# Two layers of graph attention: how the attention denominators are inverted, which buffers setup and FF1 use, and when the rows are loaded

## The chip, the cores and the metric

The kernel runs on one core of one Trainium2 chip. Its engines each run their own queue of instructions: TensorE (PE; its weight loads are listed apart as PEld), VectorE (DVE), ScalarE (ACT), GpSimd (POOL) and SyncE (SP), which here only issues DMA transfers. The time is the device time of one execution in microseconds; the number compared is the median of several runs. Besides, one execution is recorded by the hardware profiler: all durations of single instructions below come from that one.

## The reference

Two layers are applied in turn to `x`, 64 sequences of 256 rows with 256 features, with a 256 x 256 adjacency of zeros and ones for each. Cut to what matters:

```python
# layer 0: two graph attentions, then norm, FF with relu, norm
def _gat(h, adj, W, a):
    Wh = h @ W
    e  = leaky_relu(Wh @ a[:256] + swapaxes(Wh @ a[256:], 1, 2), 0.2)
    return softmax(where(adj > 0, e, NEG), axis=1) @ Wh
h = layernorm(x + _gat(_gat(x, adj, W1, a1), adj, W2, a2))
x = layernorm(h + relu(h @ w_ff1 + b_ff1) @ w_ff2 + b_ff2)

# layer 1: relational attention, 8 heads of 32, then norm, FF with gelu, norm
attn = softmax(q @ k.T / sqrt(32))                 # per head
out  = sum_r (attn * (adj == r)) @ (x @ Wv[r])     # r = 0, 1 occur
x = layernorm(x + out @ Wo + bo)
x = layernorm(x + gelu(x @ W1 + b1) @ W2 + b2)
```

The part that the change is mostly about is the softmax of layer 1. The kernel does not divide the weights by their sum; it multiplies the weighted values by the inverse of the sum at the end.

## The kernel before

**Tiling.** A pair of sequences (G = 2) is one unit of work: 512 rows, kept as four tiles of 128 rows, or with the features on the 128 partitions and the 512 rows along the columns. There are 32 pairs (NG). A general path stands behind a check at the end (`checks`, `good`, `bad`) and is not entered with these inputs; the sums kept in `low`, `lowg`, `high` and `other` feed that check.

**Turns.** The pairs are in a pipeline of three. In `turn(y, x, z)` (32 times, with y, y + 1, y + 2) pair y goes through layer 1, pair x = y + 1 through the feed-forward of layer 0, and pair z = y + 2 through the two graph attentions. In the second last turn there is no z, in the last neither x nor z; there the code goes another way (`to_features` on TensorE in place of `normed_features`; the last products of pair 30 are cut in pieces, called by `piece()` inside the last turn).

**Order.** TensorE and SP follow the order of the program text (`manual_schedule`); a planner orders VectorE, ACT and POOL by its own estimate of costs, each queue then running strictly in its order. `behind(...)` puts what it encloses after a marked instruction of the same engine.

**Attention of layer 1.** A pair has four quads of heads, (sequence b, group m), two for each sequence. `weighted` (L988 to L999) makes scores, exponentials `e`, masked exponentials `ea` and the row sums `es`. `applied` accumulates values in the PSUM tile `po` (L1009) and the sums in `zo` (L1012). The stationary operand of the latter is a matrix of ones with 32 columns, so the 32 partitions of one head in `zo` hold the same number: of each 32 rows of `zo` only one is distinct. `divided` (L1017, L1018), after the second quad of a sequence, takes the reciprocal of all 128 x 512 elements and multiplies `po` by it into `oT`, which the output product (L760) reads. `noted` (L1025) sums the reciprocals on ACT into a column of `low`. In a turn with a z, the projection of pair z (L707) stands on TensorE between the output products of the two sequences.

**FF1 of layer 1.** `hidden_seven` (L833 to L850) computes the product in seven quarter products, Strassen fashion. Partial results from one PSUM bank are copied by ACT (L839) into a tile `cp` (slots of tag `ea`), and VectorE adds the other bank to it into the quarter of `h1` where it belongs (L843); then gelu works on `h1` in place.

**Buffers.** A tile belongs to a tag with a number of slots (`bufs`); a new tile waits until the oldest in its tag has been read. `y`, the rows of a pair, has five slots and is loaded at the head of `load_x`, before the eight transfers of `xq`, in the turn before the pair becomes z. The scores `s` of the graph attentions have two slots. At setup `columns` (L491 to L496) loads short vectors as rows on ACT's queue, transposes them on TensorE and copies them out; it is called twice, for the attention vectors (`ga`) and for ten others (`cols`), with rows in the one slot of tag `rz`. Three bias rows (L503, L628) are loaded by SP into that same slot, one after the other, and added by POOL.

**Other lines that the prediction names.** L457, L459: rows and adjacency of the first two pairs. L577 to L580: POOL's sums of weights. L588: products that fold a shift into a bias. L595: scaling of weights on POOL. L646 and L647: transposes of `to_features` on TensorE and ACT's copies of them. L661, L680: the transposes of `normed_features` on VectorE and its transfers. L699: `checked`. L716: the score rows. L730 to L736: the masked softmax of the graph attention. L749: its first sums. L777: the power in the normalisation. L798, L892: the feed-forward of layer 0. L913, L918: the pieces of the last product and their additions. L1034: the transposition of `xq`. L1099: the store of the output.

## Time and profile before

| | us |
|---|---|
| median of 3 runs | 3161.23 |
| lowest, highest | 3158.11, 3163.35 |
| the profiled execution | 3159.55 |
| its span, first to last instruction | 3157.6 |
| mean granted TensorE clock in it | 0.991 |

From the page, the span in 40 equal slices of 79 us: each digit is the busy share of a slice in tenths, and PEclk the granted clock of TensorE in the same way.

```profile
PE   7999999999999999999999999999999999999997
...
DVE  3577777777777777777777777777777777777765
ACT  4355544545544545545545545545445555445442
POOL 2121111111111111111211111211111211111200
PEclk8999999999999999999999999999999999999998
DMA  5011111111111111111111111111111111111000
```

The middle of the kernel is even; the first slices and the last differ in every row. In the lists of groups, a row has the source line, the engine, the operation, the tiles written and read, their shapes and the count; then busy time and mean duration, then the idle time of the engine just before and what ended it. In a timeline a row begins with the start and the duration.

### The profile page before, as it was taken

To read this page: it belongs to the slowest core of one execution; us is meant where nothing else is said; L and a number is where in the kernel's file an instruction comes from. 1 tells how busy PE (TensorE), PEld (TensorE's weight loads), DVE (VectorE), ACT (ScalarE), POOL (GpSimd) and SP (SyncE) were. 2 spreads that over 40 slices of the span, in tenths; PEclk is the share of its full clock that TensorE was granted. 3 is DMA by queue.
4 is the path that set the end of the run, shared out by engine and by line. 5 is a ranking of instruction groups with operands and counts; after the bars stand their busy time and mean duration, and the time that the engine had idled before them with its cause. 6 is when DMAs were issued, how large, how long until landed. Compare 5 with 4: busy or idle time off the path is not lost. (4 is left out here: it accounts for less than half of the span.)

```text
span 3157.6 us, 50461 instructions
## 1 busy us (share of the span) xinstructions
PE 3097.2 (98%) x19120; PEld 2199.1 (70%) x19120; DVE 2329.8 (74%) x4146; ACT 1548.6 (49%) x3088; POOL 521.2 (17%) x757
## 2 busy tenths in 40 slices
PE   7999999999999999999999999999999999999997
PEld 5577766677766777666777666777666777666755
DVE  3577777777777777777777777777777777777765
ACT  4355544545544545545545545545445555445442
POOL 2121111111111111111211111211111211111200
PEclk8999999999999999999999999999999999999998
DMA  5011111111111111111111111111111111111000
GB/s 145 19 36 26 41 31 38 43 36 25 39 35 37 40 35 28 36 38 37 36 35 32 34 39 38 36 28 39 32 41 38 36 27 40 31 39 28 16 12 15
DMA packets 428536, 113.38 MB, mean 36 GB/s; under 512 B 364760, under 2 KB 427648, under 8 KB 428288
## 3 DMA queue, kind: packets, MB, share of 16 engines
q1 hardware_dynamic: 417952, 102.66, 14.7%
q10 hardware_dynamic: 9280, 6.39, 0.7%
q8 instruction: 153, 2.51, 0.3%
q0 software_dynamic: 1056, 1.05, 0.1%
q14 instruction: 95, 0.78, 0.1%
HBM read 57.04 MB, written 16.78 MB: 23 GB/s over the span
## 5 line engine op out<-in xcount | busy, mean ns | idle before, releaser
L798 PE MATMUL h1p<-hT,wf 128*128 128x512 f32 x992 | 450.6, 602 | 0.0
L892 PE MATMUL yfp<-wf,h 128*128 128x256 f32 x2048 | 447.3, 379 | 0.0
L892 PEld LDWEIGHTS yfp<-wf,h 128*128 128x128 f32 x2048 | 386.9, 190 | 51.9 <-issue 0.5
L781 ACT ACTIVATE y<-y,nm,rs 128x256 f32<-128x256 f32 x512 | 272.9, 597 | 237.9 <-DVE nm L778 237.9
L994 ACT ACTIVATE e<-sp 128x512 f32<-128x512 f32 x512 | 264.3, 602 | 250.4 <-PE sp L988 238.1
L996 DVE TENSOR_TENSOR ea<-e,aT 128x1024 f32<-128x1024 f32 x256 | 312.2, 1261 | 51.1 <-ACT e L994 47.0
L798 PEld LDWEIGHTS h1p<-hT,wf 128*128 128x128 f32 x992 | 180.8, 190 | 228.6 <-issue 183.3
L776 POOL TENSOR_SCALAR rs<-mv 128x4 f32<-128x4 f32 (+1 forms) x130 | 54.8, 421 | 1692.0 <-DVE mv L775 1686.4
L800 ACT ACTIVATE h<-h1p,cols 128x512 f32<-128x512 f32 x256 | 176.7, 690 | 222.3 <-PE h1p L798 222.3
L678 POOL COPY hT<-yt 32x256 f32<-32x256 f32 x248 | 241.2, 973 | 185.0 <-DVE yt L661 177.3
L1017 DVE RECIPROCAL rz<-zo 128x512 f32<-128x512 f32 x64 | 214.7, 3354 | 58.5 <-PE zo L1012 58.5
L661 DVE STREAM_TRANSPOSE yt<-y 128x256 f32<-128x256 f32 x368 | 162.6, 442 | 97.1 <-ACT y L781 88.6
L972 PE MATMUL vp<-wv,hT 128*128 128x512 f32 x480 | 214.0, 599 | 0.0
L774 DVE BATCH_NORM_STATS2 st<-y 128x6 f32<-128x256 f32 x512 | 195.8, 415 | 4.5
L843 DVE TENSOR_TENSOR h<-h1a,cp 128x512 f32<-128x512 f32 x192 | 130.9, 682 | 64.6 <-PE h1a L833 61.0
L988 PEld LDWEIGHTS sp<-q,k 32*128 32x128 f32 x2048 | 92.7, 184 | 109.6 <-issue 72.8
L961 ACT ACTIVATE q<-qp,cols 128x512 f32<-128x512 f32 x64 | 43.3, 677 | 255.1 <-PE qp L959 255.1
L709 ACT COPY xp<-xpp 128x260 f32<-128x260 f32 x128 | 47.9, 376 | 244.9 <-PE xpp L707 244.9
L972 PEld LDWEIGHTS vp<-wv,hT 128*128 128x128 f32 x480 | 88.7, 190 | 110.4 <-issue 103.2
L789 DVE TENSOR_TENSOR y<-y,rb 128x1024 f32<-128x1024 f32 (+1 forms) x130 | 162.1, 1248 | 3.3
L788 DVE TENSOR_TENSOR y<-y,rg 128x1024 f32<-128x1024 f32 (+1 forms) x130 | 157.3, 1211 | 9.2 <-PE h1T0p L646 3.6
L918 DVE TENSOR_TENSOR y<-yf,y 128x256 f32<-128x256 f32 x224 | 93.3, 417 | 84.8 <-PE yf L913 84.7
(209 smaller groups left out, 5762.3 us busy)
## 6 DMA issues: line engine op xcount, KB each, us to landing
hT<-yt SPq DMA_DIRECT2D x918, 32.0 KB, 1.9
y<-in_x_dram SPq DMA_DIRECT2D x32, 512.0 KB, 4.1
xq<-in_x_dram SPq DMA_DIRECT2D x240, 64.0 KB, 2.3
aq<-in_adj_dram SPq DMA_DIRECT2D x240, 64.0 KB, 2.4
out_dram<-y SPq DMA_DIRECT2D x30, 512.0 KB
hT<-yt ACTq DMA_DIRECT2D x186, 32.0 KB, 1.9
wf<-in_L_gnn_w_ff_dram SPq DMA_DIRECT2D x2, 1024.0 KB
w<-in_L_gnn_W_dram SPq DMA_DIRECT2D x2, 1024.0 KB
```

What stands on the lines that cost most here:

```text
L661: mark["transposed"] = nc.vector.transpose(yt[:, :, :, t].rearrange("p q k r -> p k q r"), xn[:, t].rearrange("p (k q c) -> p k q c", k=KB ...
L678: nc.gpsimd.tensor_copy(to, at)
L774: nc.vector.bn_stats(st[:, t, :], y[:, t, :])
L781: mark["normed"] = nc.scalar.activation(y[:, t, :], y[:, t, :], AF.Identity, bias=nm[:, t:t + 1], scale=rs[:, t:t + 1])
L789: nc.vector.tensor_add(y, y, b_[:, None, :].to_broadcast(list(y.shape)))
L798: nc.tensor.matmul(ps, wi[:, k, f * P:(f + 1) * P], hT[k], start=(k == 0), stop=(k == KB - 1))
L800: nc.scalar.activation(h1[:, f, :], ps, func, bias=bi[:, f:f + 1])
L892: nc.tensor.matmul(ps[:, i * F:(i + 1) * F], h1[:, k, t * P:(t + 1) * P], wo_[:, k, :], start=(k == 0), stop=(k == FB - 1))
L972: nc.tensor.matmul(ps, hT[k][:, t * P:(t + 1) * P], wvf[:, k, :], start=(k == 0), stop=(k == KB - 1))
L994: mark[f"exp{b * KB + m}"] = nc.scalar.activation(e[:, a, :], ps[a], AF.Exp, scale=isd)
L996: nc.vector.tensor_tensor(ea[:, a:a + 2, :], e[:, a:a + 2, :], ab[:, None, :].to_broadcast([P, 2, NB * N]), ALU.mult)
L1017: nc.vector.reciprocal(rz, zo)
```

## The change

`divided` no longer takes the reciprocal of all of `zo`. It transposes `zo` in blocks of 32 x 32, so that the equal rows of a head become equal columns; takes the reciprocal of the first column of each block, 16 in all, into a small tile `rq`; and transposes back, reading each of the 16 columns 32 times. The sum for the check is now an addition of `rq` to `low` (128 x 16) on POOL; `noted` is gone.

```diff
-    low = const.tile([P, NG * G], F32, name="low")
+    low = const.tile([P, KB * N // 32], F32, name="low")
+    nc.gpsimd.memset(low, 0.0)
...
     def divided(u, b, po, zo, oT):
         rz = work.tile([P, KB * N], F32, tag="rz", name=f"rz{u}_{b}", bufs=1)
-        nc.vector.reciprocal(rz, zo)
+        rq = work.tile([P, KB * N // 32], F32, tag="rq", name=f"rq{u}_{b}")
+        nc.vector.transpose(rz, zo)
+        nc.vector.reciprocal(rq, rz.rearrange("p (n r) -> p n r", r=32)[:, :, 0])
+        nc.gpsimd.tensor_add(low, low, rq)
+        nc.vector.transpose(rz.rearrange("p (n r) -> p n r", r=32),
+                            rq[:, :, None].to_broadcast([P, KB * N // 32, 32]))
         mark[f"divided{b}"] = nc.vector.tensor_tensor(
             oT[:, :, b * N:(b + 1) * N], po.rearrange("p (m n) -> p m n", m=KB),
             rz.rearrange("p (m n) -> p m n", m=KB), ALU.mult)
-        return rz
-
-    def noted(u, b, rz):
-        nc.scalar.activation(rz, rz, AF.Identity, accum_out=low[:, u * G + b:u * G + b + 1])
```

Setup tiles get buffers of their own: the rows of `ga` lie in tag `k`, those of `cols` in tag `q`, and the three bias rows side by side in `v`. Of the pair of copies in `to_features`, the second goes to VectorE. The scores `s` of the first two pairs lie in tag `e`, and `s` itself has one slot; in the second last turn the scratch of the last sums takes a slot of `wh` in place of the second `s`.

```diff
-    def columns(vs, name, queue):
-        rows = work.tile([P, KB * N], F32, tag="rz", name=f"{name}r", bufs=1)[:, 0:P]
+    def columns(vs, name, queue, tag):
+        rows = work.tile([P, KB, TN], F32, tag=tag, name=f"{name}r", bufs=1)[:, 0, 0:P]
...
-    for rb, v, name in ((rb1, g_bf2, "rbf2"), (rb2, t_bo, "rbo"), (rb3, t_b2, "rbt2")):
-        nc.gpsimd.tensor_add(rb, rb, row(v, name, work.tile([P, KB * N], F32, tag="rz", name=name, bufs=1)[:, :F]))
+    rows = work.tile([P, T, 2 * F], F32, tag="v", name="rows", bufs=1)
+    for n, (rb, v) in enumerate(((rb1, g_bf2), (rb2, t_bo), (rb3, t_b2))):
+        nc.gpsimd.tensor_add(rb, rb, row(v, None, rows[:, n, :F]))
...
-            nc.scalar.copy(dst[:, k, :], ps)
+            (nc.vector.tensor_copy if k else nc.scalar.copy)(dst[:, k, :], ps)
...
-        s = work.tile([P, T, N], F32, tag="s", name=f"s{name}")
+        s = (work.tile([P, T, N], F32, tag="s", name=f"s{name}", bufs=1) if u > 1 else
+             work.tile([P, 2 * T, N], F32, tag="e", name=f"s{name}")[:, :T])
...
-            s = [work.tile([P, T, N], F32, tag="s", name=f"sq{u}_{n}") for n in range(2)]
+            s = [work.tile([P, T, N], F32, tag="s", name=f"sq{u}", bufs=1),
+                 work.tile([P, T, WX], F32, tag="wh", name=f"wq{u}")[:, :, :N]]
```

In `hidden_seven` the tile `cp` is gone: ACT copies a partial result straight into the quarter of `h1` to which it will belong, and VectorE adds the other bank to it in place.

```diff
-        cp = work.tile([P, HPB, NB * N], F32, tag="ea", name=f"cp{u}_{l}")
...
-        def copied(h, n, ps):
-            c = cp[:, 2 * h + n, :]
-            mark["copied"] = nc.scalar.copy(c, ps)
-            return c
+        def copied(h, o, b, ps):
+            mark["copied"] = nc.scalar.copy(out(h, o, b), pair(ps))
...
+        def added(h, o, b):
+            mark["added"] = nc.vector.tensor_tensor(out(h, o, b), pair(one[h]), out(h, o, b), ALU.add)
...
         for h in halves:
             product(two[h], h, s1, moving(0), True)
-            p5[h] = copied(h, 1, two[h])
+            copied(h, 1, 1, two[h])
...
             product(two[h], h, s4, quarter[1][1], False)
-            copied(h, 0, two[h])
+            copied(h, 0, 1, two[h])
```

The rows `y` have four slots in place of five. They are loaded by `load_rows`, which stands after the store of the pair that has ended (`finish`), while `load_x` loads `xq` alone. The check of the first two adjacencies moves behind the sums of the second graph attention of pair 0.

```diff
-        y = io.tile([P, T, F], F32, tag="y", name=f"y{u}", bufs=5)
-        nc.sync.dma_start(y, x[G * u:G * (u + 1)].rearrange("b (c p) f -> p (b c) f", p=P))
...
+    def load_rows(u):
+        y = io.tile([P, T, F], F32, tag="y", name=f"y{u}", bufs=4)
+        nc.sync.dma_start(y, x[G * u:G * (u + 1)].rearrange("b (c p) f -> p (b c) f", p=P))
+        g[u].update(y=y)
...
         if waiting:
             finish(*waiting.pop(), 0, G, ("summed1", "exp2"), ("divided0",))
+        if z + 1 < NG:
+            load_rows(z + 1)
...
-        for u in range(2):
-            checked(u, g[u]["aq"])
         second_sums(0, on_tensor=True)
+        with behind("summed"):
+            for u in range(2):
+                checked(u, g[u]["aq"])
```

## The prediction

> **What bounds the kernel now.** I read the busy shares first, then who waited for whom with TensorE alone, then the two ends of the timeline.

> From the page, the busy share of each engine:

> ```profile
> PE 3097.2 (98%) x19120; PEld 2199.1 (70%) x19120; DVE 2329.8 (74%) x4146; ACT 1548.6 (49%) x3088; POOL 521.2 (17%) x757
> ```

> A busy TensorE is not proof that it is the bound, so its waits come next (total us, times, longest):

> ```profile
> PE colsp L495 <- DMA wo<-in_L_gnn_Wo_dram: 8.3, 1, 8.3
> PE gap L495 <- DMA gar<-in_L_gnn_a_dram: 6.8, 1, 6.8
> PE sp L988 <- ACT k L961: 5.1, 30, 0.2
> PE qp L959 <- ACT h2T L647: 4.7, 2, 2.7
> PE yop L760 <- DVE q L1018: 4.7, 2, 2.9
> ```

> All of TensorE's waits together come to some 50 us, and only one recurs by the turn: 0.17 us for the keys, 30 times. The others happen once or twice. So in the 30 middle turns (95.3 us each: the values start at 1076.99 in one turn and at 2983.42 twenty turns later) nothing but TensorE's own work decides, and the change touches no steady matmul. **What the change can gain lies in the first 120 us and the last 140.** The reciprocal, 214.7 us of VectorE, is not worth 214.7 us, nor is any part of it that falls inside a turn.

> **The division.** The old row against its neighbours (the page's groups and the groups by shape; busy, mean ns):

> ```profile
> L1017 DVE RECIPROCAL rz<-zo 128x512 f32<-128x512 f32 x64 | 214.7, 3354 | 58.5 <-PE zo L1012 58.5
> L736 DVE RECIPROCAL z<-z 128x4 f32<-128x4 f32 x64 | 10.9, 170 | 0.1
> L1034 DVE STREAM_TRANSPOSE xT<-xq 128x1024 f32<-128x1024 f32 x30 | 37.0, 1234 | 0.0
> L661 DVE STREAM_TRANSPOSE yt<-y 128x256 f32<-128x256 f32 x368 | 162.6, 442 | 97.1 <-ACT y L781 88.6
> ```

> A reciprocal costs (3354-170)/508 = 6.27 ns a column, so 16 columns cost 170 + 12 x 6.27 = 0.25 us. A transpose costs (1234-442)/768 = 1.03 ns a column, so 512 columns cost 0.71 us. Neither row reads PSUM or a broadcast source. Bounds: 0.62 (half the 1024 row) and 1.23 (no faster than the 1024 row); I take 0.71, since the same VectorE addition takes 0.68 from PSUM at 512 (L843) and follows the same slope. New: 0.71 + 0.25 + 0.71 + 0.06 between them = 1.73 against 3.35, **1.62 us less**, 64 times, 104 us of VectorE. [...] By the rows the fixed part is about 0.15 us (256 columns 0.415, 512 columns 0.68), so two more instructions cost 0.3 us, which is in my sum[...].

> In a middle turn this is worth nothing. Around the second division of a turn:

> ```profile
> 1110.86 3.36 DVE L1017 RECIPROCAL rz<-zo 128x512 f32<-128x512 f32 x1 [1.76 <-PE zo L1012]
> ...
> 1114.68 0.68 DVE L1018 TENSOR_TENSOR q<-po,rz 128x512 f32<-128x512 f32 x1
> ...
> 1115.99 1.89 PE L760 MATMUL yop<-wo,q 128*128 128x256 f32 x8
> ```

> An addition of rows (L763, 0.63 us) stands between the two. The product is ready at 1115.36 and TensorE comes at 1115.99, straight from the next pair's projection (L707): 0.6 us to spare already.

> The last two turns have no next pair to project, and there the division is exposed. Second last turn:

> ```profile
> 3017.28 3.36 DVE L1017 RECIPROCAL rz<-zo 128x512 f32<-128x512 f32 x1 [4.19 <-PE zo L1012]
> ...
> 3021.10 0.68 DVE L1018 TENSOR_TENSOR q<-po,rz 128x512 f32<-128x512 f32 x1
> ...
> 3021.93 3.65 PE L760 MATMUL yop<-wo,q 128*128 128x256 f32 x8 [2.86 <-DVE q L1018]
> ```

> 1.62 of the 2.86 us goes. The wait costs more than itself. The stages (length, busy times, PEclk before the last two columns):

> ```profile
> 3017.00:3022.00 5.00, 2.14 (x13) 1.54 (x9) 4.71 (x4) 0.12 (x1) 0.00 (x0) 1.00 0.00 0
> 3022.00:3025.40 3.40, 3.40 (x8) 2.71 (x9) 0.66 (x4) 0.60 (x2) 0.00 (x0) 0.50 0.00 0
> ```

> After the gap the granted clock is 0.50 for 3.4 us: eight matmuls take 3.65 us here and 1.89 in a middle turn, 1.76 more. [...] The row shows half speed after 2.86, while 1.86 us of idleness (3103.9) left the next stage at 1.00. With 1.2 us left, I count the 1.76 as gained.

> The tail, summed:
> - second last turn: 1.62 + 1.76 = 3.4
> - last turn, first division (3085.56): L918 stands behind the reciprocal, and the scores wait 3.37 us for the bank that it frees. 1.62, plus the half-clock stage after it (3.63 against 1.95 us for 16 matmuls): 3.3
> - last turn, second division (3101.12): TensorE waits 1.86; 1.62
> - feature copies on two engines: the h3T pair takes 1.05 us on ACT and its first reader waits for both; 0.5. The h2T31 pair stands behind gelus and the first product needs only the first half: 0. The other pairs (xT, h1T, h2T0): 0 to 0.5 each, 0 counted

> **Tail 8.8 us**, between 4 (clock stages stay) and 11.

> **The start.** TensorE stands from 14.6 to 22.8 for the transposition of the vectors, and ACT's queue issues those ten loads:

> ```profile
> 7.06 0.24 ACTq L491 DMA_DIRECT2D colsr<-in_L_gnn_g_ln_dram  x1
> ...
> 20.57 0.28 ACTq L491 DMA_DIRECT2D colsr<-in_L_gnn_b_dram  x1
> ```

> The first could not go before 7.06, because it shares its buffer with the two attention vectors, read at 6.78. With buffers apart it can go at 2.3, behind their issue: 4.7 us earlier. Four go by 7.94, four from 12.41, one at 17.45 and the last at 20.57, with stops while earlier transfers land on a DMA system 0.77 to 0.93 busy; a buffer doesn't cure those. Ends: 0 (the later stops decide alone) and 8.2 (the whole gap). I take 4.7, the stop that the buffer causes. A gap of 3.5 us would remain, so I count none of the half-clock stretch after it (0.50 from 23.0 to 28.5, at most 2.9 us). One thing follows: VectorE's masked products at 35.05 take 1.49 us for what takes 0.42 elsewhere, beside POOL's weight sums (34.83 to 40.7), and TensorE then waits 3.45 us at 39.9. Moved forward 4.7 us, some of them leave POOL's way; between 0 and 3.4, I take 1. **Start 5.7 us**, from 0 to 14.5.

> **Costed at nothing.**
> - The sum into low moves from ACT (0.65 + 0.22, 64 times) to POOL (0.25, by L737's 0.24). POOL is 17% busy; behind it stands the next normalisation's rs, some 10 us later. Exposed, 0.25 a time.
> - FF1's copies into h1 are the same copies with another destination; h1's last readers (L892) precede L833 on TensorE. A copy into a strided target costs between 0.58 and 0.69 (L843 writes such a one): 0.1 x 6, on an ACT 49% busy.
> - One s buffer: the old scores are read by L749 until 1050.7, and the new ones need L716, at 1052.31 behind it on TensorE. The first pairs' scores rotate through two slots of e as they did through two of s; the last sums' scratch takes the free slots of wh.
> - y rows later: SP issues out at 1103.33, must now await its landing before y (one buffer fewer), and the six feature transfers on SP stand behind. They come at 1124.06; a y load lands in 4.1 us, the store presumably in about as much, so some 12 us are free; if the store took over 16, the transfers and with them FF1 would be late. xq goes 3 us earlier, past y.
> - The bias rows in three slots of v: rbo waits until 41.64 and rbt until 45.66 today for POOL; nothing on TensorE's path waits there (POOL reaches the scaling at 51.59 and waits for L588).
> - checked (1.22 twice) moves behind the sums at 66; VectorE idles 1.47 us at 69.1 and POOL's result is late; at worst 1 us.

> **Sum:** 3157.6 - 8.8 - 5.7 = 3143.1 span. The profiled execution took 3159.55, near the median of 3161.23; 3161.2 - 14.5 = **3147**.

> **Rivals.**
> 1. Tail only: the later loads stop on transfers, the start gives 0. 3161.2 - 8.8 = 3152. For it: two of the four stops come after 12 us. Against: the first four would be long landed.
> 2. The start closes whole: 8.2 + 2.9 + 3.4 + 8.8 = 23.3, 3138. For it: the adjacency lands 11.5 us after its issues at 1.48 and 2.84, so by 15; against: the busy DMA.
> 3. Nothing to measure, about 3158: the planner, which orders VectorE, ACT and POOL by its own costs, puts the shorter work elsewhere in both ends.
> 4. **Slower:** transposes from PSUM are dear. From 1110.86 to 1115.83 a middle turn has 4.97 us (0.15 for the handover); less 0.25, 0.63 and 0.69 leaves 3.4 for two transposes. Above 1.7 us each, TensorE stalls in every turn. At 2.47 (twice the 1024 row) 1.5 us x 30, and 2 x 1.5 in the last turns: about 3209. Against: 1.7 is 2.4 times the slope's price.

> **How the numbers follow.** 0.2% of this kernel, 6.3 us, is what can be told from no change. Forecast 0.54 (3142 to 3152 by itself); tail only 0.15; whole start 0.12; nothing 0.09; slower 0.10. Faster takes the first three less 0.04 for a tail below 6.3: 0.77; same 0.13; slower 0.10. The range, 3137 to 3157, holds the first three and leaves the last two out.

> **What would show it.** Right: no reciprocal of 512 columns, transposes of 0.6 to 0.8; the 2.86 and 3.37 waits under 1.9 and no 0.50 stage behind them; colsp near 18; middle turns still 95.3. Wrong: colsp at 22 or later; a middle turn off 95.3 by over 0.2; a wait of TensorE that comes 30 times besides the one for the keys.

## The result and the profile after

Four runs of each kernel on one chip, taken in turns:

| | before | after |
|---|---|---|
| median | 3162.29 us | 3145.5 us |
| lowest to highest | 3158.11 to 3163.41 | 3140.3 to 3152.31 |
| ratio, 95% interval | | **0.9951** [0.9927, 0.9974] |
| the profiled execution, span | 3157.6 us | 3150.7 us |

The ratio is worth 15.5 us of 3162.3, between 8 and 23. The profiled execution of the changed kernel took 3152.31 us and is the slowest of its four; that matters below. Lines of code are those of the changed kernel from here on: `divided` is L1025 to L1030, the columns L495 to L500, the copies of `to_features` L652, the output product L766, the scores L993, the queries L964.

First the busy share of each engine, from the page:

```profile
PE 3100.9 (98%) x19120; PEld 2200.3 (70%) x19120; DVE 2234.9 (71%) x4280; ACT 1513.4 (48%) x2954; POOL 532.2 (17%) x822
```

VectorE lost 95 us of work, ACT 35, and TensorE is as busy as it was. Then the waits of TensorE (total us, times, longest):

```profile
...
PE rows L721 <- ACT hp L757: 5.2, 2, 4.1
PE qp L964 <- ACT h2T L652: 5.1, 2, 2.7
PE sp L993 <- ACT k L966: 5.1, 30, 0.2
...
PE sp L993 <- DVE y L923: 1.8, 1, 1.8
PE qp L964 <- DVE h2T L652: 1.8, 1, 1.8
...
PE yop L766 <- DVE q L1030: 0.8, 1, 0.8
```

The list that had `colsp` at its head (8.3 us) no longer has it at all, and `yop` fell from 4.7 us to 0.8. New in it is a wait of the queries for a copy on VectorE (`qp` for `h2T` on DVE), 1.8 us. The wait that comes 30 times is the old one, for the keys. The wait of `rows` for `hp` has grown to 5.2; before, `rows` waited as follows:

```profile
PE rows L716 <- ACT xp L709: 3.5, 1, 3.5
...
PE rows L716 <- ACT hp L751: 1.7, 2, 1.2
```

The new instructions of the division, by shape:

```profile
L1025 DVE STREAM_TRANSPOSE rz<-zo 128x512 f32<-128x512 f32 x64 | 45.7, 713 | 87.9 <-PE zo L1017 87.9
L1028 DVE STREAM_TRANSPOSE rz<-rq 128x512 f32<-128x512 f32 x64 | 45.5, 711 | 2.2
L1026 DVE RECIPROCAL rq<-rz 128x16 f32<-128x16 f32 x64 | 16.2, 253 | 2.2
```

And where it is exposed, the second last turn, in the timeline (start, duration):

```profile
3015.01 0.72 DVE L1025 STREAM_TRANSPOSE rz<-zo 128x512 f32<-128x512 f32 x1 [5.18 <-PE zo L1017]
...
3016.80 0.69 DVE L1030 TENSOR_TENSOR q<-po,rz 128x512 f32<-128x512 f32 x1
3017.41 0.68 DVE L769 TENSOR_TENSOR y<-yop,y 128x512 f32<-128x512 f32 x1
```

The product starts 1.79 us after the division begins; before, 3.82 us. Of these 2.03 us, 1.62 are the shorter division; the rest comes from the addition of rows (L769), which stood between reciprocal and product and now stands behind the product.

I cut each trace at the first values of the first and of the second last turn. The **start** is what lies ahead of the first cut, the **middle** is 30 turns, the **end** is the rest; the expectations below call start and end FRONT and TAIL. With them, how long TensorE's granted clock was 0.50 within start and end (these three traces have their first record of the clock at 14.0 to 14.8 us):

```
us                      colsp  start   middle   end     half clock: start, end
before                  22.82  123.42  2860.00  174.20       34.1  23.0
after                   14.37  121.80  2859.41  169.45       34.1  26.6
after, second execution 13.94  118.57  2859.68  162.75       27.3  10.6
```

The middle gave nothing. The two executions of the changed kernel are the same instructions, yet 9.7 us apart, and all of it lies in the two ends, where they differ by 22.8 us of half clock.

**The start** gained 8.45 us at `colsp` and kept only 1.6 of it in this execution (4.9 in the other). Before, the columns were transposed here:

```profile
22.82 0.28 PE L495 MATMUL colsp<-ident,colsr 32*128 32x32 f32 x1 [8.27 <-DMA wo<-in_L_gnn_Wo_dram]
```

Where the gain was given back, in the timeline of the changed kernel:

```profile
2.34 0.28 ACTq L495 DMA_DIRECT2D colsr<-in_L_gnn_g_ln_dram  x1
...
9.71 0.28 ACTq L495 DMA_DIRECT2D colsr<-in_L_gnn_b_dram  x1
...
14.37 0.28 PE L499 MATMUL colsp<-ident,colsr 32*128 32x32 f32 x1
...
27.04 5.46 PE L712 MATMUL xpp<-gwe,xT 128*128 128x260 f32 x16 [2.16 <-ACT xT L652]
...
34.20 2.96 DVE L736 SCALAR_TENSOR_TENSOR s<-s 128x512 f32<-128x512 f32 x2 [6.64 <-ACT s L733]
35.42 3.19 POOL L633 TENSOR_TENSOR rb<-rb,rows 128x256 f32<-128x256 f32 x3
...
37.08 0.95 DVE L739 SCALAR_TENSOR_TENSOR s<-s,aT 128x256 f32<-128x256 f32 x1
...
42.69 1.02 PE L721 MATMUL rows<-ident,hp 128*128 128x128 f32 x3 [4.08 <-ACT hp L757]
...
111.42 0.68 DVE L652 COPY h2T<-h2T0p 128x512 f32<-128x512 f32 x1
112.24 5.12 PE L964 MATMUL qp<-h2T,wq 128*128 128x512 f32 x6 [1.75 <-DVE h2T L652]
```

All ten loads are issued by 9.71, where the last came at 20.57. Then three waits: `xpp` for a feature copy of the second pair, 2.16 us (VectorE was waiting for the weights `wv`, which arrive at 23.13, with the softmax of the first pair behind them); `rows` for the softmax of the second pair, 4.08, whose two operations of L736 take 2.96 us beside POOL's weight sums (until 35.4) and bias additions; and `qp` for VectorE's half of the copy `h2T0`, 1.75, which stands behind the two affine steps of pair 0, the transposes of pair 1 and the first affine step of pair 1.

### The profile page after: what moved, and what is told of

Same layout as the page of the kernel before. It is cut to its first block, busy times and chain, and to the rows that moved or that the text cites. A ratio compares the mean times of both kernels' runs of the same rounds, so it can differ in the third digit from the quotient of the medians.

```text
span 3150.7 us, 50482 instructions
## 1 busy us (share of the span) xinstructions
PE 3100.9 (98%) x19120; PEld 2200.3 (70%) x19120; DVE 2234.9 (71%) x4280; ACT 1513.4 (48%) x2954; POOL 532.2 (17%) x822
## 3 DMA queue, kind: packets, MB, share of 16 engines
q0 software_dynamic: 1056, 1.05, 0.1%
## 5 line engine op out<-in xcount | busy, mean ns | idle before, releaser
L850 DVE TENSOR_TENSOR h<-h1a,h 128x512 f32<-128x512 f32 x192 | 131.0, 682 | 64.2 <-PE h1a L838 59.8
L993 PEld LDWEIGHTS sp<-q,k 32*128 32x128 f32 x2048 | 93.2, 184 | 108.1 <-issue 72.8
L1004 DVE TENSOR_TENSOR es<-e 128x1024 f32<-128x1024 f32 x128 | 155.8, 1217 | 0.0
```

## The experiments

Each kernel was timed in five rounds against the kernel before on its own chip; ratios are to that one. "Start" and "end" are those of the one profiled execution.

**The changed kernel again**, as the measure of what one execution can tell.

> The changed kernel once more, for a second profile and a second comparison. Markers used for all runs here: FRONT is the start of the first values product of the first turn (123.4 us before, 121.8 in the first profile after); TAIL is from the first values product of the second last turn to the end of the span (174.2 before, 169.5 after); the 30 turns between took 2860.0 and 2859.4. Theory A (the waits that the change removes are the same in every execution, and only the half-clock stages behind the remaining waits differ): colsp again at 14.4, second last yop wait again 0.8, last-turn scores wait 1.8; FRONT and TAIL differ from the first profile only by stretches at PEclk 0.50, up to 3.4 us each. Ratio to before 0.993 to 0.997. Rival (the first profile was an accident of the transfers): colsp somewhere between 14 and 20.

Measured: 3142.95 us, 0.9949 [0.9936, 0.9963], start 118.57, end 162.75. The gain stands, at 16.1 us; the single executions differ by more than most of what follows, so medians decide.

**The division alone, on the kernel before.** Everything else as before.

```diff
-        nc.vector.reciprocal(rz, zo)
+        rq = work.tile([P, KB * N // 32], F32, tag="rq", name=f"rq{u}_{b}")
+        nc.vector.transpose(rz, zo)
+        nc.vector.reciprocal(rq, rz.rearrange("p (n r) -> p n r", r=32)[:, :, 0])
+        nc.gpsimd.tensor_add(low, low, rq)
+        nc.vector.transpose(rz.rearrange("p (n r) -> p n r", r=32),
+                            rq[:, :, None].to_broadcast([P, KB * N // 32, 32]))
```

> Before, with the new division alone. Theory A (the division acts in the tail alone): FRONT 123.4 within 1; TAIL 165 to 170; middle 2860; in all 5 to 9 us less, ratio 0.997 to 0.9985. Rival B (the gain is at the start and the division is hidden everywhere): TAIL 174 and ratio 1.000. Rival C (ACT's freed time or VectorE's matters in each turn): the middle falls by over 3 us.

Measured: 3151.95 us, 0.9973 [0.9964, 0.9981]: 8.5 us of 3159.43, between 6 and 11. `colsp` is at 22.71 as before, the end is 165.33 against 174.20, 8.9 us less, which is the median's gain. The start is a miss: 120.49, where 123.4 within 1 was expected. No line of the setup was edited, and two executions of one kernel differ by 3.2 us there (the table above), so this one trace does not show that the division gains anything at the start.

**The setup buffers alone, on the kernel before** (the rows of `ga`, of `cols` and the three bias rows).

```diff
-        rows = work.tile([P, KB * N], F32, tag="rz", name=f"{name}r", bufs=1)[:, 0:P]
+        rows = work.tile([P, KB, TN], F32, tag=tag, name=f"{name}r", bufs=1)[:, 0, 0:P]
...
-        nc.gpsimd.tensor_add(rb, rb, row(v, name, work.tile([P, KB * N], F32, tag="rz", name=name, bufs=1)[:, :F]))
+        nc.gpsimd.tensor_add(rb, rb, row(v, None, rows[:, n, :F]))
```

> Before, with the setup buffers alone (columns in k and q, bias rows in v). Theory A (the shared slot caused the 8.3 us wait): colsp at 14.4 to 15, TAIL 174 within 2, FRONT 115 to 121, ratio 0.997 to 0.9995. Rival B (it takes the other edits as well, for instance the copies on VectorE, to start early): colsp at 18 or later, FRONT 123.

Measured: 3151.61 us, 0.9974 [0.9967, 0.9982]: 8.2 us, between 5.7 and 10.4. End 173.93, which is the kernel before's. `colsp` in the traces of the two parts, first the division alone, then the buffers alone:

```profile
22.71 0.28 PE L496 MATMUL colsp<-ident,colsr 32*128 32x32 f32 x1 [8.51 <-DMA colsr<-in_L_gnn_b_dram]
```

```profile
14.25 0.31 PE L495 MATMUL colsp<-ident,colsr 32*128 32x32 f32 x1
```

The start is 114.25, 9.2 us earlier than before, with 23.9 us at half clock within it and not 34.1: here nothing of the gain at `colsp` was given back. The two parts add up to 16.7 us, and the whole change is worth 16.1.

**Both of them and nothing else.**

> Before, with the new division and the setup buffers, and nothing else of the change (rows loaded early, five y slots, FF1 through cp, two s slots, both copies on ACT). Theory A (these two parts are the whole gain, the other edits bring nothing): ratio 0.9945 to 0.9955, the sum of the two alone (0.27 and 0.26%), colsp at 14.0 to 14.4, second last yop wait 0.8. Rival B (the other edits bring a share, in the middle or at the ends): ratio 0.996 or more. Rival C (the other edits cost): 0.9935 or less, FRONT 3 us or more under 118.6.

Measured: 3141.4 us, 0.9947 [0.9933, 0.9960]. FF1 in place, the one `s` buffer, the later rows, the later check and the split of the copies add nothing that this can see, with some 4 us of uncertainty on either side. The traces are less even: the start is 115.22 here and 114.25 with the buffers alone, against 121.80 and 118.57 in the changed kernel, and the end is 164.61 against 169.45 and 162.75. So the give-back shown above is not the work of the earlier columns alone. Here the queries do not wait for VectorE, and the longest wait for `hp` is 2.94 us (2.25 with the buffers alone), not 4.08. Which of the further edits lengthened it was not tested.

**Both copies of `to_features` on ACT again.**

```diff
-            (nc.vector.tensor_copy if k else nc.scalar.copy)(dst[:, k, :], ps)
+            nc.scalar.copy(dst[:, k, :], ps)
```

> The changed kernel with both copies of to_features on ACT again. Theory A (the h2T0 copy that went to VectorE stands there behind the affine of pair 0 and costs 1.8 us of waiting and a longer half-clock stage): the wait of qp for VectorE gone, FRONT 2 to 5 us earlier than with the change, TAIL 0 to 1 longer for the h3T copies. Rival B (ACT's copy would stand there as long as VectorE's): FRONT within 1 of the changed kernel's, TAIL 0.5 longer.

Measured: 3143.45 us, 0.9948 [0.9934, 0.9961]. The wait of the queries for VectorE is gone and the start is 116.27, 2.3 to 5.5 us earlier than in the two executions of the changed kernel; the median doesn't show it. Either the split gains in the end about what it costs at the start, or both are too small to be seen; this stays open.

**Three repairs of the start, one by one.** The subtraction of `wv` behind the softmax of the second pair:

```diff
-    nc.vector.tensor_tensor(wv[:, :, 1, :], wv[:, :, 1, :], wv[:, :, 0, :], ALU.subtract)
...
+        with behind("inverted"):
+            nc.vector.tensor_tensor(wv[:, :, 1, :], wv[:, :, 1, :], wv[:, :, 0, :], ALU.subtract)
```

> The changed kernel, with VectorE's two subtractions on wv and rbv put behind the second pair's inverse of the graph softmax. Theory A (in the changed kernel VectorE idles 5.8 us at 17 to 23 for the load of wv, and the first pair's softmax stands behind it): that idleness goes, the first leaky product starts at 22.4 instead of 24.1, the wait of xpp for the xT copy shrinks from 2.2 or 3.0 to under 1.5, FRONT 1 to 3 us earlier than 118.6 to 121.8. Rival B (ACT's own order holds the xT copy): the wait stays above 2, FRONT unchanged.

Measured: 3142.86 us, 0.9949 [0.9936, 0.9963]. `xpp` waits 0.72 us in place of 2.16 and the start of this execution is 116.82, but the median shows no gain; the wait for `hp`, 3.72 us, is still there.

POOL's weight sums and bias additions behind the scaling of the weights:

```diff
-        w2s.extend(seven_out(w2, "w2"))
+        with behind("weighed"):
+            w2s.extend(seven_out(w2, "w2"))
...
+        with behind("weighed"):
+            for rb, r in biases:
+                nc.gpsimd.tensor_add(rb, rb, r)
```

> The changed kernel, with POOL's sums of w2 and its three bias additions put behind later scalings of weights. Theory A (VectorE's products run at a third of their speed beside POOL, and the wait of TensorE for hp, 4.1 and 3.6 us, comes of it): the products at 34 to 41 take 0.42 and 0.7 us, the wait for hp falls to under 1.5 us, the half-clock stage at 41.3 to 48 goes, FRONT 3 to 6 us earlier than the changed kernel's. Rival B (the wait is a matter of ACT's order alone): the products are fast and the wait stays above 3.

Measured: 3138.39 us (3137.44 to 3141.51), 0.9936 [0.9922, 0.9949], against 3142.86 (3139.53 to 3144.42) of the repair above on the same chip: 4.5 us less, with ranges that overlap a little. In its timeline, at the place shown above:

```profile
34.37 1.42 DVE L741 SCALAR_TENSOR_TENSOR s<-s 128x512 f32<-128x512 f32 x2 [6.64 <-ACT s L738]
35.76 0.43 DVE L744 SCALAR_TENSOR_TENSOR s<-s,aT 128x256 f32<-128x256 f32 x1
...
38.51 1.12 POOL L599 TENSOR_SCALAR wf<-wf,cols 128x1024 f32<-128x1024 f32 x1 [10.43 <-PE bf1sp L592]
...
39.54 0.87 PE L726 MATMUL rows<-ident,hp 128*128 128x128 f32 x3 [0.75 <-ACT hp L762]
```

and, later, the three bias additions:

```profile
46.51 2.09 POOL L615 TENSOR_TENSOR rb<-rb,rows 128x256 f32<-128x256 f32 x3
```

With POOL idle until 38.5, the same two operations take 1.42 us and not 2.96, a masked sum 0.43 and not 0.95, and TensorE waits 0.75 and not 4.08. The contention was real: before, it had met the first pair (a masked sum of 1.49 us at 35.05), and with the earlier columns it meets the second. POOL suffers as well: its three bias additions take 3.19 us there and 2.09 here, where VectorE is idle until 48.50. What the two engines contend for was not shown.

The copy `h2T0` wholly on VectorE, with pair 0's affine steps behind it:

```diff
-            (nc.vector.tensor_copy if k else nc.scalar.copy)(dst[:, k, :], ps)
+            mark["features"] = (nc.vector.tensor_copy if k or name == "h2T0" else nc.scalar.copy)(dst[:, k, :], ps)
...
-        affine(g[0]["y"], rg2, rb2)
+        with behind("features"):
+            affine(g[0]["y"], rg2, rb2)
```

> The changed kernel, with both h2T0 copies on VectorE and the affine of pair 0 held behind them. Theory A (the copies can go at 104 and 105, and stand behind other work on both engines): qp waits under 0.5 us instead of 2.4 and 1.8, the half-clock stage there shrinks from 10.2, FRONT 4 to 8 us earlier than the changed kernel's. Rival B (the second pair's normalisation is late instead and TensorE waits for it later): FRONT gains, and the middle loses as much.

Measured: 3142.33 us, 0.9947 [0.9933, 0.9961]. A miss: the queries wait 3.72 us for VectorE. Pair 1's transposes and the first of its affine steps were put ahead of the copies, and nothing in the edit held them back.

**All three repairs together.**

> The three edits together on the changed kernel. Theory A (what the start gained by the early columns was given back to waits that these remove): FRONT 105 to 111, ratio to before 0.990 to 0.993. Rival B (each wait removed uncovers the next, and the gains do not add up): FRONT 113 or later, ratio 0.9935 to 0.995.

Measured: 3136.83 us, 0.9931 [0.9917, 0.9944], start 112.71. With the third repair still failing (3.72 us), this is what POOL's move gives and little more.

**The order of `h2T0` mended in the program text**, with the first two repairs: its transposes and copies stand between pair 1's last sums and pair 1's normalisation.

```diff
-        second_sums(1)
-        g[0]["hT"] = to_features(g[0]["y"], "h2T0")
+        second_sums(1, between=lambda: g[0].update(hT=to_features(g[0]["y"], "h2T0")))
```

> The changed kernel with wv's subtractions and POOL's sums later, as in the run of all three, but with the h2T0 copies split as in the change and the whole of the copying traced between pair 1's last sums and its normalisation, so that the planner places them ahead of it on both engines. Theory A (the copies wait for nothing but their place in the queue): qp waits under 0.8 us, FRONT 105 to 110, ratio 0.991 to 0.993. Rival B (the planner puts them late again): qp waits 2 us or more, FRONT 112 to 115.

Measured: **3133.99 us, 0.9918 [0.9904, 0.9931]**, start 105.50. In its timeline:

```profile
92.51 0.69 DVE L658 COPY h2T<-h2T0p 128x512 f32<-128x512 f32 x1 [0.57 <-PE h2T0p L657]
94.64 6.42 PE L970 MATMUL qp<-h2T,wq 128*128 128x512 f32 x8
```

Both copies are done by 93.2, beside the bias products that run to about 94.7, and the queries follow with no wait, if still mostly at half clock (0.56 on average from 94.60 to 101.00; eight take 3.60 us at full). This version is faster than the kernel before and than the two parts alone: its runs lie between 3129.76 and 3134.43, those of the two parts, on the same chip, between 3140.51 and 3144.91. What the order of `h2T0` adds to the first two repairs can be read from the wait (3.72 us to none) and not from the times: against the run of all three repairs, on another chip, the intervals overlap.

**Matmuls that nobody reads, put into three gaps of this version**, to see whether work in a gap keeps the half clock away: at the start ahead of the transposes `h1T0` of the first pair, and in the last turn ahead of the queries and ahead of `h3T`. First 6, 5 and 4 of them.

```diff
+    def filler(name, n):
+        ps = bank(name)
+        for _ in range(n):
+            nc.tensor.matmul(ps, ident, wf1[:, 0, 0:512], start=True, stop=True)
...
+            filler("f1", 6)
...
+                filler("f2", 5)
...
+            filler("f3", 4)
```

> The kernel of the run before, with matmuls whose result nobody reads put into three of TensorE's waits: six of 512 columns ahead of the h1T0 transposes, five behind the h2T31 transposes, four ahead of the h3T31 transposes. Theory A (a wait of TensorE costs itself and then a half-clock stage of 3.4 to 6.8 us, and the stage is set by how idle TensorE was just before): the stages behind these three go; qp of the last turn takes 3.6 us for eight where it took 5.4 to 6.8, TAIL 2 to 5 us shorter, FRONT 1 to 3. Rival B (the clock falls whatever TensorE does there, by the time since the last stage): stages stay, and the time is the same or longer by what the fillers overrun.

Measured: 3134.8 us, 0.9923 [0.9909, 0.9936]. They were twice as long as meant: each is two MATMUL instructions of 0.45 us at full clock, so 5.40, 4.46 and 3.60 us stood in gaps of 3.6, 2.7 and 2.35. The half-clock stages behind the first two gaps went. Ahead of the products of `h3T` a new wait of 2.61 us stood, with a stage of 3.4 us behind it where there had been one of 6.8. That the overrun took the gain is likely, but not shown.

Then 3, 2 and 2:

> The kernel of h2_first with 3, 2 and 2 matmuls that nobody reads (0.90 us each at full clock: 2.7, 1.8 and 1.8 us) in the three gaps of 3.6, 2.7 and 2.35 us: at the start ahead of the scores of the first pair, and in the last turn. In the first trial of this they were twice as long and overran the gaps. Theory (a half-clock stage follows a gap of TensorE, and work of any kind in the gap keeps it away): the remaining idleness is about 0.9 us in each, the stages behind them stay away, nothing is overrun; the time from the values of the second last turn to the end 160 to 163.5 us, start of the first values 102 to 105.5 us, ratio to before 0.990 to 0.9912. Rival (the stages come from something else than the gap before them, or move to the next gap): end part 164 to 167 us as in h2_first, ratio 0.9915 to 0.992.

Measured: 3133.76 us, 0.9917 [0.9903, 0.9931], start 104.25, end 162.79. In the last turn:

```profile
3080.76 1.88 PE L654 MATMUL f<-wf,ident 128*128 128x512 f32 x4
3083.28 0.33 PE L662 MATMUL h3T31p<-ident,y 128*128 128x128 f32 x1 [0.63 <-ACT y L798]
...
3086.30 2.08 PE L849 MATMUL h1b<-h3T,w 128*128 128x256 f32 x4 [0.78 <-DVE h3T L663]
```

The gap of 2.35 us is 0.63 now, with no overrun, and yet the four products at 3086.30 take 2.08 us (1.03 at full clock): a stage of 3.4 us came all the same, in place of one of 6.8. The parts in this execution are where the theory put them, the median is the rival's. No gain is shown.

## Why the prediction was right

Predicted 3147 us, a gain of 14.5; measured 3145.5 and 3142.95, gains of 15.5 and 16.1. By its steps:

- **The middle gives nothing: right.** 30 turns took 2859.41 us against 2860.00, although the division's VectorE time fell from 214.7 to 107.4 us.
- **The division costs 1.73 us: right**, 0.71 + 0.25 + 0.71 and gaps. Neither PSUM (713 ns) nor the broadcast source (711 ns) costs anything against the 0.71 us worked out from rows with neither, which ends the slower rival (above 1.7 us a transpose). One term was too small: exposed, the product comes 2.03 us earlier and not 1.62, because the addition between them moved behind it.
- **The tail, 8.8 us: right in the median** (the division alone gave 8.5), less so in its parts. The waits are as summed: `yop` 2.86 to 0.77, the scores 3.37 to 1.79, the last `yop` 1.86 to 0 (0.75 in the second execution), `h3T` 1.51 to 0.78. That is 5.5 to 6.3 us, where the prediction had 5.4. The clock behind them was counted as 3.4 us and is not one number: the half-clock stage after `yop` is gone in every trace with the new division, the one after the scores, which the prediction counted as gone, is there in 4 of 12. In the profiled execution the end gained 4.8 us, in the second 11.4.
- **The start, 5.7 us: the sign right, the terms wrong.** The step "I take 4.7, the stop that the buffer causes" was mis-sized: the stops after it went too, and `colsp` came at 14.37 and not "near 18", 8.45 us earlier, as rival 2 had it. A wait was missing from the sum: `xpp` for a copy behind the arrival of `wv`, 2.16 us in the changed kernel and 3.03 with the buffers alone, where it had been 0.20. The step "I take 1" for leaving POOL's way brought nothing in the changed kernel, since the contention moved on to the second pair, where it cost 3.3 us; with the buffers alone the waits behind it fell from 3.94 us (3.45 and 0.49) to 2.25. And the step "the other pairs (xT, h1T, h2T0): 0 to 0.5 each, 0 counted" missed the queue: 1.75 us in `h2T0`, in the whole change alone. The errors have opposite signs, so that the total came out near the forecast is in part luck. The buffers alone measured 8.2 us, between 5.7 and 10.4, with the 5.7 at its edge.
- **Costed at nothing: right as far as the medians tell**, which is to some 4 us. The two parts alone are as fast as the whole, but in the traces their start is 3.4 to 6.6 us earlier, so a cost of the other edits there is not excluded. For the rows: SP issues `out` at 1004.35 and `y` at 1007.27, after a wait of 2.5 us, and its next transfer at 1026.68.

Not settled: how much of the start's give-back is waits and how much clock. A wait and the half-clock stage behind it were only taken away together.

## What to carry to other kernels

Before an engine's costliest instruction is made cheaper, look for the places where somebody waits for it: 107 us of VectorE were worth 8.5 us here, all of them in the last two turns. A transfer that comes earlier moves everything behind it (of 8.45 us at `colsp`, 1.6 stayed in the profiled execution), so read which engines it will meet there; the one repair that paid by itself, with 4.5 us, was to take POOL out of VectorE's way. And a single profiled execution does not size an edit at the ends of this kernel, where the clock differs from one execution to the next (60.7 us at half clock in one, 37.9 in the other).

## What the runs showed of the hardware

**The half-clock stages lie on a fixed grid.** The same wait of 1.79 us stands ahead of the same matmuls in both executions of the changed kernel. The stages after it (length, busy times, PEclk before the last two columns), in the slower one:

```profile
3083.10:3089.90 6.80, 6.80 (x33) 5.99 (x34) 4.30 (x5) 2.06 (x4) 0.00 (x0) 0.50 0.00 0
```

and in the second:

```profile
3077.00:3083.00 6.00, 5.99 (x66) 5.07 (x70) 4.53 (x6) 2.06 (x4) 0.00 (x0) 1.00 0.00 0
```

33 matmuls in 6.8 us against 66 in 6.0. The first of them, after the wait, in the one and in the other:

```profile
3083.02 2.06 PE L993 MATMUL sp<-q,k 32*128 32x256 f32 x10 [1.79 <-DVE y L923]
```

```profile
3077.01 1.12 PE L993 MATMUL sp<-q,k 32*128 32x256 f32 x10 [1.79 <-DVE y L923]
```

```
idle in the cell, us     cells   next cell at half clock
under 1.2                1409       0
1.2 to 1.6                 35       2
1.6 to 2.0                 39      24
2.0 and more               42      42
```

So in these traces it is not the length of a wait that decides but how much idleness falls into one cell: about half of it (1.6 to 2.0 of 3.4 us). A wait of 3.37 us gave a stage in both traces that have it, one of 2.86 in both, one of 2.7 (the queries of the last turn) in 7 of 12, one of 1.79 in 4 of 12, one of 0.77 in none of 12: the same wait, ahead of the same matmuls, with and without a stage. Between 1.6 and 2.0 us of idleness the table does not decide. Counting one-column products as work spoils the table: 21 of the 68 stages then follow a cell with under 1.2 us of idleness, where none does above. They don't seem to keep the clock up. The way back is narrower: of 39 cells at half clock with 0.8 us or more of idleness, all were followed by another. That this offset makes the spread of the medians is argued, not shown: the runs that were only timed have no trace.
